# A decoder layer's last stage in 7 tiles of 128 tokens, six batches routed earlier, and two weight loads re-ordered

## The chip, the cores and the metric

The kernel runs on one core of a Trainium2 chip. A core has five engines that run their own instruction queues side by side: TensorE (PE, matmul and transpose), VectorE (DVE), ScalarE (ACT), GpSimd (POOL) and SyncE (SP, which mainly issues DMAs). The metric is the device time of one execution in microseconds (us), as the median of several runs; lower is better.

## The reference, cut to what matters

One decoder layer, post-norm, all in float32, for 8 batches of 112 tokens with 256 channels:

```python
x = _layernorm(x + self_attention(x))        # 16 heads of 64
x = _layernorm(x + cross_attention(x, ctx))  # 16 heads of 16, 375 context tokens per batch, one mask
x = _layernorm(x + ffn(x))

def ffn(x):                                  # x: 896 tokens x 256
    idx = argmax(x @ router.T)               # one of 8 experts for each token
    y = expert[idx](x)                       # silu(x @ gate.T) * (x @ up.T) @ down.T, 512 hidden
    ys = silu(x @ w_gate_s.T) * (x @ w_up_s.T) @ w_down_s.T   # the shared expert, every token
    return y + ys
```

The layernorm has no weights: it subtracts the mean and divides by sqrt(variance + 1e-5).

## The kernel before, in words

**Stages.** The work goes batch by batch. In step s, the self-attention of batch s and the cross-attention of batch s-1 are interleaved; step 0 has no cross-attention, and the last step (table LAST) has the cross-attention of batch 7 and then the feed-forward part. For that the tokens are sorted by expert: the place of each token is counted, its row is sent by an indirect DMA on POOL into a DRAM tensor `xs_d` (`to_places`, L670), each expert's first 128 rows are loaded back (`load_tiles`, L873), go through the expert (`ExpertTile`: `turn` transposes, `gate_up`, `down`), and the output plus its residual goes to `y_d` (L840). A ninth, small tile takes what is beyond 128 rows of an expert; which expert and row that is, SP reads from registers that it loads from memory (L793, L881). At the end the rows of each batch are gathered from `y_d` (`from_places`, L685), the shared expert's product is added, the norm is taken and the rows are written out.

**The order is written by hand.** The scheduler is switched off; each step runs through a table of words, and each engine gets its instructions in that order. A letter is a piece of work: S and E are scores and exponentials of the cross-attention (S, a group of four heads), T its transposes, W and U the weights, V the product with the values, F (or f, of batch 7) the four finishing pieces; s, e, w, t, v, o, n, q are those of the self-attention and of the query projection; k, u, c are projections for later batches. A + or - chooses DVE or ACT for the copy out of PSUM. In LAST, a and b are the shared expert's gate and up products of the first half of the tokens, h those of the second, p (or r) and P (or R) the two halves of the routing (r, R: batches 0 to 5; p, P: batches 6 and 7), L the loads of the sorted rows, A, B, C the turn, gate/up and down of tile 0 to 8, x the count of the rows beyond 128, Y, D, Z the gather, sum and norm of the end. `down(t)` also issues the loads of expert t+4's weights on SP, and for t = 4 the loads of the ninth tile's row number, rows and weights (`load_expert`, L877).

**The start.** SP and ACT's queue issue the first loads (L138 to L148): the first columns of q's weights on ACT, x and k's weights on SP.

**Buffers.** PSUM has two tiles each of three kinds: `sc` (two banks; a cross-attention group S takes both, a self-attention group s takes one), `pt` (transposes) and `mm`. Four sets of expert weights are in flight.

**Every DMA that starts with `load(...)` is issued by SP**, in program order; SP waits for the semaphores of a DMA before it issues it, and what comes later in its queue waits behind.

**The end.** `r`, `mv` are laid out by batch, 112 tokens on the partitions. A batch's norm is one DVE instruction (L242) with the mean and the reciprocal deviation, which POOL makes with a power (L238).

Of the kernel before, what the change touches and what calls it, by code (L numbers as in the profile page):

```python
# [25 lines left out]


STEP = """
S0 E0 k2 s0 u1- e0 T00+ F1 w0 c0 T02- S1 E1 u0- T01+ t00+ W0 s1 T10- T11- e1 c1 T12+ U0+ w1 V0 S2 c4
k3- t01- F2 F3 k0 t10+ t11- E2 v0+ v1- S3 T20+ E3 T22- o W1 T30- c2 n F4 T31+ k1- q1 U1- c3 T21+ q2  # L30
T32- V1
"""
STEP6 = """
S0 E0 c0 s0 c1 e0 T00+ T02- S1 c4 E1 w0 W0 T01- s1 u1- T10- T11- e1 u0+ U0- w1 t00- F1 T12- c3 t01-
S2 t10+ t11- V0 E2 v0+ v1- S3 T20- E3 F2 o n T21- W1 T30- c2 F3 T32- q1 F4 T22- T31- q2 U1+ V1
"""
STEP7 = """
S0 E0 c0 s0 c1 e0 S1 T00- E1 T01+ s1 c4 T02- T10- W0 U0- e1 w0 T12- w1 T11- S2 V0 t00+ t01- E2 F1
t10- v0- t11+ F2 S3 T20- v1+ E3 F3 o T30- n W1 T22- c3 T32- T21+ F4 q1 c2 T31- U1- q2 V1
"""  # L40
FIRST = """
k6 k4 u0- k5- k7+ s0 e0 s1 k3- u3- k1- e1 k2 u1- k0 w0 w1 t00+ t01+ u2- t10+ t11- v0+ v1+ z o c0 n
c1 c3 q1 c4 q2 c2
"""
LAST = """
S0 E0 F1 a2- S1 E1 a1- T00+ b0- T02+ F2 W0 T01- S2 T10+ T12- b1- E2 T11+ U0+ S3 V0 F3 E3 T20+ a3+
T22+ T21+ a0+ W1 T30- T31- F4 T32- U1- r V1 f1 R f2 b2+ f3 f4 b3- p P L0 h2 L1 h0 h1 A0 g1 A1 B0 L2
B1 A2 x C0 B2 A3 A4 C1 C2 B3 B4 A5 A6 C3 B5 C4 B6 A7 C5 B7 g0 A8 C6 B8 C7 C8 Y0 Y1 Y2 Y3 D0 Y4 Y5 D1
h3 Z0 Y6 D2 Z1 Y7 D3 Z2 D4 Z3 D5 Z4 D6 Z5 D7 Z6 Z7
"""  # L50


# [1 line left out]
def decoder_layer(  # L54
# [19 lines left out]
    E, _, H = upT.shape  # L74
    KH = H // P
    NTT = NT // P
    HB = B // 2
    HT = HB * S

    NG = 4  # L80
    NOV = (NT - 1) // P
# [2 lines left out]
    const = ctx.enter_context(tc.tile_pool(name="const", bufs=1))  # L84
# [12 lines left out]
    def m_tile():  # L97
        return ps_m.tile([P, 512], F32, tag="mm", name="mm")
# [10 lines left out]
    ac = sa.enter_context(tc.tile_pool(name="ac", bufs=1))  # L109
# [5 lines left out]
    wo1 = ac.tile([P, NC, D], F32, name="wo1")  # L115
    bo1 = ac.tile([S, D], F32, name="bo1")
    xres = const.tile([S, B, D], F32, name="xres")
    r = const.tile([S, B, D], F32, name="r")
    mv = const.tile([S, B, 2], F32, name="mv")
    x2T = const.tile([P, KD, NT], F32, name="x2T")  # L120
    lgs = const.tile([S, B, E], F32, name="lgs")
    rt = const.tile([P, KD, E], F32, name="rt")
# [1 line left out]
    load = nc.sync.dma_start  # L124
# [3 lines left out]
    def load_w(start, n, c, width):  # L128
        start(out=wqkv[n][:, :, bass.ds(c, width)], in_=w_v[:, :, bass.ds(n * INNER + c, width)])
# [10 lines left out]
        load(out=xT_sb[:, k, 0 : 2 * S], in_=xT_v[:, k, 0 : 2 * S])  # L140
    load_w(A.dma_start, 0, P, P)
    load_w(load, 1, 0, 256)
    load_w(A.dma_start, 0, 256, 256)
    load_w(load, 1, 256, 256)
    for n in range(3):
        load_w(load, n, 512 if n < 2 else 0, 512)
# [64 lines left out]

    xs_d = tc.dram_tile([E * NT, D], F32, name="xs_d")
    y_d = tc.dram_tile([E * NT, D], F32, name="y_d")
    fill_sb = const.tile([P, D], F32, name="fill_sb")
    G.memset(fill_sb, 0.0)

    cap = xc.tile([S, S2], F32, name="cap")
# [9 lines left out]
    def stats(dst, src):  # L227
        st = small.tile([P, 6], F32, tag="st", name="st")
        n = src.shape[0]
        V.bn_stats(st[:n], src)  # L230
        V.bn_aggr(dst, st[:n])

    def rstd_of(var):

        n = var.shape[0]
        rs = small.tile([P, 1], F32, tag="rs", name="rs")
        V.tensor_scalar(rs[:n], var, EPS, None, ALU.add)  # L237
        G.tensor_tensor(rs[:n], rs[:n], mhalf[:n], ALU.pow)  # L238
        return rs[:n]

    def normalize(dst, src, mean, rs):
        V.tensor_scalar(dst, src, mean, rs, ALU.subtract, ALU.mult)  # L242
# [8 lines left out]
    def copy(on, dst, src):  # L251

        (V.tensor_copy if on == "+" else A.copy)(dst, src)  # L253

    def product(out_, pairs):
        for i, (lhsT, rhs) in enumerate(pairs):
            nc.tensor.matmul(out_, lhsT, rhs, start=(i == 0), stop=(i == len(pairs) - 1))  # L257
# [74 lines left out]
    class SelfAttention:  # L332
# [57 lines left out]
        def project(self, on):  # L390
            b = self.b
            G.tensor_tensor(xres[:, b, :], xres[:, b, :], bo1, ALU.add)
            ps = m_tile()
            product(ps[:S, :D], [(self.aoT[:, c, :], wo1[:, c, :]) for c in range(NC)])
            V.tensor_tensor(r[:, b, :], ps[:S, :D], xres[:, b, :], ALU.add)
            stats(mv[:, b, :], r[:, b, :])
            self.rs = rstd_of(mv[:, b, 1:2])

        def norm(self, on):
            b = self.b  # L400
            normalize(xres[:, b, :], r[:, b, :], mv[:, b, 0:1], self.rs)


    class CrossAttention:
# [124 lines left out]
        def finish_3(self):
            transposed(x2T[:, :, bass.ts(self.b, S)], xres[:, self.b, :])  # L530
# [60 lines left out]
    fc = ctx.enter_context(tc.tile_pool(name="fc", bufs=1))  # L591
# [12 lines left out]
    swd = fc.tile([P, KH, D], F32, name="swd")  # L604
# [19 lines left out]
    def shared_half(hc):
        ug = sc_tile()
        for i, w in enumerate((swu, swg)):
            product(
                ug[:, i, :HT], [(w[:, k, bass.ts(hc, P)], x2T[:, k, HT:]) for k in range(KD)]
            )
        sg = fp.tile([P, 512], F32, tag="sg", name="sg", bufs=3)  # L630
        A.activation(sg[:, :HT], ug[:, 1, :HT], AF.Silu)
        V.tensor_tensor(hS1[:, hc, :], ug[:, 0, :HT], sg[:, :HT], ALU.mult)

    rstds = {}

# [2 lines left out]
        A.activation(raw["g"][:, h, :], raw["g"][:, h, :], AF.Silu)  # L638
        V.tensor_tensor(raw["u"][:, h, :], raw["u"][:, h, :], raw["g"][:, h, :], ALU.mult)

    def last_sum(b):

        h = raw["u"] if b < HB else hS1
        ps = m_tile()
        product(
            ps[:S, :D], [(h[:, hc, bass.ts(b % HB, S)], swd[:, hc, :]) for hc in range(KH)]
        )
        V.tensor_tensor(r[:, b, :], ps[:S, :D], r[:, b, :], ALU.add)
# [11 lines left out]
    def small_tile(name, shape=None, dt=F32):  # L660
        return fc.tile(shape or [S, B], dt, name=name)
# [5 lines left out]
    place_i = small_tile("place_i", None, I32)  # L667
# [14 lines left out]
            tc.declare_no_dep(i.ins, other.ins, reason="distinct places")  # L682
        sent.append(i)

    def from_places(b):  # L685
        G.indirect_dma_start(  # L686
            out=r[:, b, :],
            out_offset=None,
            in_=y_d[:, :],
            in_offset=bass.IndirectOffsetOnAxis(ap=place_i[:, b : b + 1], axis=0),  # L690
            bounds_check=E * NT - 1,
            oob_is_err=False,
        )
# [105 lines left out]
    class ExpertTile:  # L799
# [32 lines left out]
        def down(self):  # L832
            ps = m_tile()
            n = self.x.shape[0]
            product(
                ps[:n, :D], [(self.hT[:, hc, 0:n], self.w[2][:, hc, :]) for hc in range(KH)]
            )
            y = fp.tile([P, D], F32, tag="y", name="y", bufs=3)
            V.tensor_tensor(y[:n], ps[:n, :D], self.x, ALU.add)
            load(out=y_d[bass.ds(self.rows, n), :], in_=y[:n])  # L840
# [63 lines left out]
    for b in range(B):
        raw_pieces[f"Y{b}"] = lambda on, b=b: from_places(b)
        raw_pieces[f"D{b}"] = lambda on, b=b: last_sum(b)
        raw_pieces[f"Z{b}"] = lambda on, b=b: last_norm(b)
# [20 lines left out]

    with tc.If(n_more > 0):
        more(0)  # L930
        for b in range(B):
            from_places(b)
            last_sum(b)
            last_norm(b)


# [50 lines left out]
```

## Time and profile before

| what | us |
|---|---|
| median of 3 runs (lowest to highest) | 417.23 (416.98 to 417.66) |
| the profiled execution's own time | 417.91 |
| its span in the profile | 416.1 |
| PE busy / weight loads | 401.2 / 312.9 |
| DVE / ACT / POOL busy | 240.0 / 187.5 / 75.3 |
| PE's first product of q starts / the first waits of the routing (A0) / last expert matmul ends | 4.27 / 339.95 / 388.8 |

The profile is of one execution. A line of the timeline gives start, duration, engine, line of the kernel, operation, output <- inputs, the count of merged instructions, and in brackets how long the engine had been idle and what ended that. A line of waits gives who waited for whom: total us, times, longest. "SPq" and "POOLq" are the sequencers of SP and POOL. A line of a table by stretches gives, for a window of the span, its length, then for PE, weight loads, DVE, ACT and POOL the busy us and the number of instructions, then the granted share of PE's clock, the DMA engines' share and GB/s. Matmul ends are modelled, so the starts are the safer numbers. "To landing" is the time from the issue of a DMA to its completion.

### The profile page before, as it was taken

How to read it: one execution, taken by the hardware profiler on the slowest of the kernel's cores; microseconds unless marked ns; L12 is line 12 of the kernel's file. 1: busy time of each engine (PE TensorE's matmuls, PEld its weight loads, DVE VectorE, ACT ScalarE, POOL GpSimd, SP SyncE). 2: the span in 40 equal slices, each digit the busy share in tenths (PEclk: the TensorE clock that was granted, in tenths of full speed). 3: DMA queues.
4: the chain of work that ended last, by engine and by line, in shares of the span. 5: the costliest groups of instructions: out<-in, count | busy, mean ns of one | idle time of the engine just before them, and what ended most of it. 6: DMA issues, size and time to landing. Idle time of an engine off the chain costs nothing.

```text
span 416.1 us, 8528 instructions
## 1 busy us (share of the span) xinstructions
PE 401.2 (96%) x3361; PEld 312.9 (75%) x3361; DVE 240.0 (58%) x673; ACT 187.5 (45%) x476; POOL 75.3 (18%) x111
## 2 busy tenths in 40 slices
PE   8999999999999999999999999999999999999991
PEld 7877778967886887689678867867857459998670
DVE  1064685578458656855784687498487424223173
ACT  1241475456636554654566386587385221112000
POOL 3021112113012200221130112104100520000271
PEclk9999999999999999999999999999999999999996
DMA  7990497199010001001000100000694140895131
GB/s 258 303 246 0 126 370 253 32 377 334 4 39 0 2 2 38 0 2 38 1 2 2 38 2 2 1 2 2 244 372 144 46 145 2 311 356 171 49 107 56
DMA packets 38622, 46.61 MB, mean 112 GB/s; under 512 B 2213, under 2 KB 31666, under 8 KB 38578
## 3 DMA queue, kind: packets, MB, share of 16 engines
q1 hardware_dynamic: 36994, 43.66, 32.2%
q0 software_dynamic: 768, 1.84, 1.5%
q8 instruction: 28, 0.46, 0.5%
q10 hardware_dynamic: 816, 0.52, 0.4%
q14 instruction: 16, 0.13, 0.1%
HBM read 28.41 MB, written 17.60 MB: 111 GB/s over the span
## 4 chain that ended last, share of the span: by engine, by line
PE 86%; POOL 4%; issue 4%; DMA 3%; DVE 2%; ACT 0%; SPq 0%; POOLq 0%; DVEq 0%
PE mm L257 45%; PE pt L494 10%; PE sc L257 7%; PE sc L446 7%; PE mm L505 5%; PE sc L345 4%; PE mm L381 3%; PE pt L374 3%; POOL r L686 1%; DMA wk<-in_w_qkv 1%; POOL xs_d L673 1%; POOL rs L238 1%; PE pt L248 1%; DMA xs_d<-xres,place_i 1%; PE pt L809 1%
## 5 line engine op out<-in xcount | busy, mean ns | idle before, releaser
L464 ACT ACTIVATE ex<-ex,nm 112x375 f32<-112x375 f32 x128 | 76.5, 599 | 47.6 <-DVE nm L460 46.9
L460 DVE CUSTOM_DVE_ANT_0 ex<-sc,cap 112x375 f32<-112x375 f32 x128 | 63.6, 544 | 10.0 <-PE sc L446 9.6
L494 PEld LDWEIGHTS pt<-ident,ex 112*125 112x125 f32 x384 | 50.9, 188 | 17.1 <-issue 10.0
L494 PE MATMUL pt<-ident,ex 112*125 112x112 f32 x384 | 55.1, 275 | 0.1
L253 ACT COPY exT<-pt 125x448 f32<-125x448 f32 x56 | 28.3, 527 | 29.2 <-PE pt L494 29.1
L367 POOL TENSOR_TENSOR pr<-pr,den 112x896 f32<-112x896 f32 x16 | 26.9, 1683 | 79.5 <-DVE den L366 41.6
L238 POOL TENSOR_TENSOR rs<-rs,mhalf 112x1 f32<-112x1 f32 x24 | 13.4, 559 | 144.6 <-DVE rs L237 144.5
L257 PE MATMUL mm<-wv,xT_sb 128*112 128x512 f32 x64 | 31.1, 608 | 0.0
L446 PE MATMUL sc<-kc,qz 32*112 32x375 f32 x256 | 29.8, 519 | 0.1
L257 PE MATMUL mm<-wo,aoT 128*112 128x256 f32 x128 | 29.0, 380 | 0.0
L253 DVE COPY exT<-pt 125x448 f32<-125x448 f32 x40 | 24.8, 621 | 7.0 <-PE pt L494 6.5
L257 PE MATMUL mm<-xT_sb,wq 128*128 128x224 f32 x128 | 28.3, 367 | 0.0
L257 PE MATMUL mm<-xT_sb,wk 128*128 128x224 f32 x128 | 26.9, 354 | 0.9 <-DMA wk<-in_w_qkv 0.9
L257 PEld LDWEIGHTS mm<-xT_sb,wq 128*128 128x128 f32 x128 | 24.3, 198 | 3.4 <-issue 3.2
L257 PEld LDWEIGHTS mm<-xT_sb,wk 128*128 128x128 f32 x128 | 23.7, 190 | 2.6 <-PE mm L257 1.2
L257 PE MATMUL mm<-wxv,cT 128*125 128x256 f32 x96 | 25.6, 389 | 0.0
L257 PEld LDWEIGHTS mm<-wo,aoT 128*112 128x112 f32 x128 | 22.0, 177 | 4.5 <-DVE aoT L253 0.2
L464 ACT ACTIVATION_READ_ACCUMULATOR ex<-ex,nm 112x1 f32 x128 | 23.9, 187 | 0.0
L257 PE MATMUL mm<-cT,wxk 128*128 128x375 f32 x64 | 23.2, 486 | 0.0
L253 DVE COPY prT<-pt 112x448 f32<-112x448 f32 x16 | 9.8, 620 | 20.7 <-PE pt L374 20.7
L505 PE MATMUL mm<-exT,vc 125*32 125x112 f32 x768 | 21.7, 261 | 0.0
L354 DVE TENSOR_REDUCE mx<-sc 112x8 f32<-112x896 f32 x16 | 17.4, 1087 | 5.8 <-PE sc L345 5.3
(159 smaller groups left out, 647.1 us busy)
## 6 DMA issues: line engine op xcount, KB each, us to landing
xs_d<-fill_sb SPq DMA_DIRECT2D x1, 7168.0 KB, 24.0
y_d<-fill_sb SPq DMA_DIRECT2D x1, 7168.0 KB, 24.7
wg<-in_gateT SPq DMA_DIRECT2D x9, 512.0 KB, 7.2
wu<-in_upT SPq DMA_DIRECT2D x9, 512.0 KB, 7.8
wd<-in_downT SPq DMA_DIRECT2D x9, 512.0 KB, 9.7
cT<-in_ctxT SPq DMA_DIRECT2D x8, 375.0 KB, 3.6
wv<-in_w_qkv SPq DMA_DIRECT2D x2, 512.0 KB, 8.5
wo<-in_w_out SPq DMA_DIRECT2D x1, 1024.0 KB, 12.8
```

The source lines that it names most:

```text
L238: G.tensor_tensor(rs[:n], rs[:n], mhalf[:n], ALU.pow)
L253: (V.tensor_copy if on == "+" else A.copy)(dst, src)
L257: nc.tensor.matmul(out_, lhsT, rhs, start=(i == 0), stop=(i == len(pairs) - 1))
L345: nc.tensor.matmul(sc[:S, j, bass.ts(c, S)], qT[rows, 4 * g + c, self.tok], kT[rows, 4 * g + c, self.tok], start=True, stop=True,)
L354: V.tensor_reduce(self.mx, scv, AX.X, ALU.max)
L367: G.tensor_tensor(pr, pr, den.unsqueeze(3).to_broadcast([S, 2, 4, S]), ALU.mult)
L374: nc.tensor.transpose(pt[:S, bass.ts(c, S)], self.pr[g][:, j, c, :], ident[:S, :S])
L446: nc.tensor.matmul(sc[i // 2][:S, i % 2, :S2], self.qz[rows, par, c, :], kc[rows, c, :], start=True, stop=True,)
L460: V.tensor_tensor_reduce(ex[:, i, :], self.sc[g][i // 2][:S, i % 2, :S2], cap, -1.0, BIG, ALU.add, ALU.min, nm[:, i : i + 1],)
L464: A.activation(ex[:, i, :], ex[:, i, :], AF.Exp, bias=nm[:, i : i + 1], scale=-1.0, accum_out=den[:, i, g % 2 : g % 2 + 1],)
L494: nc.tensor.transpose(pt[:JT, bass.ts(i, S)], self.ex[g][:, i, bass.ts(t, JT)], ident[:S, :S])
L505: nc.tensor.matmul(av[32 * i : 32 * i + 32, 0:S], vcs[self.b % 2][:, t, 4 * c + i, bass.ds(32 * par, 32)], self.exT[2 * c + par][:, t, bas ...
```

## The change

Four things change. (1) The third piece of q's weights (columns 256 to 511) is issued by SP behind the first piece of k's, not by ACT. (2) All tables have a new order. In LAST, routing pieces r and R (the count and the six sends of batches 0 to 5) stand within the cross-attention of batch 7 and no longer behind it; x stands ahead of B1; A8 stands ahead of C5. (3) The last stage runs over 7 tiles of 128 tokens in place of 8 of 112. The places, laid out by batch, are written to a DRAM tensor and read back by tile (pieces i0 and i1, both on SP, behind A5). The split of the shared expert moves from 448 + 448 tokens to 512 + 384. (4) The norm at the end is an ACT instruction, out = r * rstd + shift, with shift = -mean * rstd from a small DVE instruction. Besides, `fill_sb` moves to a pool that is freed earlier. A tail for the case of more rows than the ninth tile holds follows suit; it isn't run with these inputs.

```diff
 STEP = """
-S0 E0 k2 s0 u1- e0 T00+ F1 w0 c0 T02- S1 E1 u0- T01+ t00+ W0 s1 T10- T11- e1 c1 T12+ U0+ w1 V0 S2 c4
-k3- t01- F2 F3 k0 t10+ t11- E2 v0+ v1- S3 T20+ E3 T22- o W1 T30- c2 n F4 T31+ k1- q1 U1- c3 T21+ q2
-T32- V1
+S0 E0 u0+ s0 u1- T00- e0 T01+ S1 E1 k3- s1 c1 T10- e1 T11- w0 k2 T02- k0 W0 w1 t00+ F1 t01- c0 t10+
+U0- c4 T12- t11+ S2 V0 E2 F2 v0+ v1+ S3 T20+ F3 E3 c3 o n W1 F4 T30- T22- k1- T21- q1 c2 T31- T32+
+q2 U1- V1
 """
...
 LAST = """
-S0 E0 F1 a2- S1 E1 a1- T00+ b0- T02+ F2 W0 T01- S2 T10+ T12- b1- E2 T11+ U0+ S3 V0 F3 E3 T20+ a3+
-T22+ T21+ a0+ W1 T30- T31- F4 T32- U1- r V1 f1 R f2 b2+ f3 f4 b3- p P L0 h2 L1 h0 h1 A0 g1 A1 B0 L2
-B1 A2 x C0 B2 A3 A4 C1 C2 B3 B4 A5 A6 C3 B5 C4 B6 A7 C5 B7 g0 A8 C6 B8 C7 C8 Y0 Y1 Y2 Y3 D0 Y4 Y5 D1
-h3 Z0 Y6 D2 Z1 Y7 D3 Z2 D4 Z3 D5 Z4 D6 Z5 D7 Z6 Z7
+S0 E0 a1- b0- T00- r S1 E1 F1 T02- a2- T01+ S2 W0 T10+ R T12- b1- E2 U0+ F2 T11+ a0+ T20- T21+ S3 E3
+V0 T22+ W1 F3 a3+ T30- T31+ F4 T32- U1- V1 f1 f2 b2+ f3 f4 p h1 P h0 h2 L0 b3- L1 A0 A1 B0 L2 x B1
+C0 A2 C1 A3 B2 B3 A4 C2 B4 C3 A5 i0 i1 A6 C4 B5 A7 g1 B6 A8 C5 B7 g0 C6 B8 C7 C8 Y0 Y1 Y2 h3 Y3 Y4
+Y5 D0 D1 Y6 D2 D3 Z0 Z1 D4 D5 Z2 Z3 Z4 D6 Z5 Z6
 """
...
-    HB = B // 2
-    HT = HB * S
+    FT = 4
+    HT, HT2 = FT * P, NT - FT * P
...
-    load_w(A.dma_start, 0, 256, 256)
+    load_w(load, 0, 256, 256)
     load_w(load, 1, 256, 256)
...
-    def last_sum(b):
-
-        h = raw["u"] if b < HB else hS1
+    def last_sum(i):
+
+
+        h, n = (raw["u"], i) if i < FT else (hS1, i - FT)
         ps = m_tile()
-        product(
-            ps[:S, :D], [(h[:, hc, bass.ts(b % HB, S)], swd[:, hc, :]) for hc in range(KH)]
-        )
-        V.tensor_tensor(r[:, b, :], ps[:S, :D], r[:, b, :], ALU.add)
-        stats(mv[:, b, :], r[:, b, :])
-        rstds[b] = rstd_of(mv[:, b, 1:2])
-
-    def last_norm(b):
-        normalize(r[:, b, :], r[:, b, :], mv[:, b, 0:1], rstds[b])
-        load(out=out[bass.ts(b, S), :], in_=r[:, b, :])
+        product(ps[:, :D], [(h[:, hc, bass.ts(n, P)], swd[:, hc, :]) for hc in range(KH)])
+        V.tensor_tensor(r[:, i, :], ps[:, :D], r[:, i, :], ALU.add)
+        stats(mv[:, i, :], r[:, i, :])
+        rstds[i] = rstd_of(mv[:, i, 1:2])
+
+    def last_norm(i):
+        shift = mv[:, i, 0:1]
+        V.tensor_scalar(shift, shift, rstds[i], -1.0, ALU.mult, ALU.mult)
+        A.activation(r[:, i, :], r[:, i, :], AF.Identity, bias=shift, scale=rstds[i])
+        load(out=out[bass.ts(i, P), :], in_=r[:, i, :])
...
+    place_2 = fc.tile([P, NTT], I32, name="place_2")
+
+    def places_out():
+        load(out=place_d[:, :].rearrange("(b s) o -> s (b o)", s=S), in_=place_i)
+
+    def places_in():
+        load(out=place_2, in_=place_d[:, :].rearrange("(i p) o -> p (i o)", p=P))
+
+    def from_places(i):
         G.indirect_dma_start(
-            out=r[:, b, :],
+            out=r[:, i, :],
...
-            in_offset=bass.IndirectOffsetOnAxis(ap=place_i[:, b : b + 1], axis=0),
+            in_offset=bass.IndirectOffsetOnAxis(ap=place_2[:, i : i + 1], axis=0),
```

More of the change, by code (lines that the diff above doesn't have):

```diff
@@ L28 @@
 STEP = """
-S0 E0 k2 s0 u1- e0 T00+ F1 w0 c0 T02- S1 E1 u0- T01+ t00+ W0 s1 T10- T11- e1 c1 T12+ U0+ w1 V0 S2 c4
-k3- t01- F2 F3 k0 t10+ t11- E2 v0+ v1- S3 T20+ E3 T22- o W1 T30- c2 n F4 T31+ k1- q1 U1- c3 T21+ q2
-T32- V1
+S0 E0 u0+ s0 u1- T00- e0 T01+ S1 E1 k3- s1 c1 T10- e1 T11- w0 k2 T02- k0 W0 w1 t00+ F1 t01- c0 t10+
+U0- c4 T12- t11+ S2 V0 E2 F2 v0+ v1+ S3 T20+ F3 E3 c3 o n W1 F4 T30- T22- k1- T21- q1 c2 T31- T32+
+q2 U1- V1
 """
 STEP6 = """
-S0 E0 c0 s0 c1 e0 T00+ T02- S1 c4 E1 w0 W0 T01- s1 u1- T10- T11- e1 u0+ U0- w1 t00- F1 T12- c3 t01-
-S2 t10+ t11- V0 E2 v0+ v1- S3 T20- E3 F2 o n T21- W1 T30- c2 F3 T32- q1 F4 T22- T31- q2 U1+ V1
+S0 E0 c0 s0 c1 e0 T00+ T01- S1 E1 c4 T02- s1 u1- T10- W0 U0- e1 w0 u0- w1 T12- T11- S2 V0 t00- t01-
+F1 t10- t11- E2 v0- v1- S3 F2 E3 T20+ T21+ o W1 n T22- c2 T30- F3 c3 q1 T31- F4 q2 U1+ T32- V1
 """
 STEP7 = """
-S0 E0 c0 s0 c1 e0 S1 T00- E1 T01+ s1 c4 T02- T10- W0 U0- e1 w0 T12- w1 T11- S2 V0 t00+ t01- E2 F1
-t10- v0- t11+ F2 S3 T20- v1+ E3 F3 o T30- n W1 T22- c3 T32- T21+ F4 q1 c2 T31- U1- q2 V1
+S0 c0 E0 s0 c1 e0 S1 T00- E1 T01+ c4 s1 W0 T02- T10- T11- e1 w0 T12- S2 c3 U0- w1 V0 t00- t01- E2 F1
+v0- t10+ F2 t11- S3 v1+ T20+ E3 T21- o T30- T22- n W1 c2 F3 T32- q1 F4 T31- q2 U1- V1
 """
 FIRST = """
-k6 k4 u0- k5- k7+ s0 e0 s1 k3- u3- k1- e1 k2 u1- k0 w0 w1 t00+ t01+ u2- t10+ t11- v0+ v1+ z o c0 n
-c1 c3 q1 c4 q2 c2
+k4 k5- k7- k6 s0 e0 s1 u2- e1 u1+ c1 u3- u0- w0 w1 k1- t00+ c3 z t01- t10- k2 t11+ v0+ v1- o n k3-
+c0 q1 c4 k0 q2 c2
 """
 LAST = """
-S0 E0 F1 a2- S1 E1 a1- T00+ b0- T02+ F2 W0 T01- S2 T10+ T12- b1- E2 T11+ U0+ S3 V0 F3 E3 T20+ a3+
-T22+ T21+ a0+ W1 T30- T31- F4 T32- U1- r V1 f1 R f2 b2+ f3 f4 b3- p P L0 h2 L1 h0 h1 A0 g1 A1 B0 L2
-B1 A2 x C0 B2 A3 A4 C1 C2 B3 B4 A5 A6 C3 B5 C4 B6 A7 C5 B7 g0 A8 C6 B8 C7 C8 Y0 Y1 Y2 Y3 D0 Y4 Y5 D1
-h3 Z0 Y6 D2 Z1 Y7 D3 Z2 D4 Z3 D5 Z4 D6 Z5 D7 Z6 Z7
+S0 E0 a1- b0- T00- r S1 E1 F1 T02- a2- T01+ S2 W0 T10+ R T12- b1- E2 U0+ F2 T11+ a0+ T20- T21+ S3 E3
+V0 T22+ W1 F3 a3+ T30- T31+ F4 T32- U1- V1 f1 f2 b2+ f3 f4 p h1 P h0 h2 L0 b3- L1 A0 A1 B0 L2 x B1
+C0 A2 C1 A3 B2 B3 A4 C2 B4 C3 A5 i0 i1 A6 C4 B5 A7 g1 B6 A8 C5 B7 g0 C6 B8 C7 C8 Y0 Y1 Y2 h3 Y3 Y4
+Y5 D0 D1 Y6 D2 D3 Z0 Z1 D4 D5 Z2 Z3 Z4 D6 Z5 Z6
 """
@@ L117, in decoder_layer @@
     xres = const.tile([S, B, D], F32, name="xres")
-    r = const.tile([S, B, D], F32, name="r")
-    mv = const.tile([S, B, 2], F32, name="mv")
+    r = const.tile([P, B, D], F32, name="r")
+    mv = const.tile([P, B, 2], F32, name="mv")
     x2T = const.tile([P, KD, NT], F32, name="x2T")
@@ L213, in decoder_layer @@
     y_d = tc.dram_tile([E * NT, D], F32, name="y_d")
-    fill_sb = const.tile([P, D], F32, name="fill_sb")
+    place_d = tc.dram_tile([NT, 1], I32, name="place_d")
+    fill_sb = ac.tile([P, D], F32, name="fill_sb")
     G.memset(fill_sb, 0.0)
@@ L394, in project @@
             product(ps[:S, :D], [(self.aoT[:, c, :], wo1[:, c, :]) for c in range(NC)])
-            V.tensor_tensor(r[:, b, :], ps[:S, :D], xres[:, b, :], ALU.add)
-            stats(mv[:, b, :], r[:, b, :])
-            self.rs = rstd_of(mv[:, b, 1:2])
+            V.tensor_tensor(r[:S, b, :], ps[:S, :D], xres[:, b, :], ALU.add)
+            stats(mv[:S, b, :], r[:S, b, :])
+            self.rs = rstd_of(mv[:S, b, 1:2])
         def norm(self, on):
             b = self.b
-            normalize(xres[:, b, :], r[:, b, :], mv[:, b, 0:1], self.rs)
+            normalize(xres[:, b, :], r[:S, b, :], mv[:S, b, 0:1], self.rs)
     class CrossAttention:
@@ L520, in finish_1 @@
             product(ps[:S, :D], [(self.xoT[:, k, :], wx["o"][:, k, :]) for k in range(KD)])
-            V.tensor_tensor(r[:, b, :], ps[:S, :D], xres[:, b, :], ALU.add)
-            stats(mv[:, b, :], r[:, b, :])
-            self.rs = rstd_of(mv[:, b, 1:2])
+            V.tensor_tensor(r[:S, b, :], ps[:S, :D], xres[:, b, :], ALU.add)
+            stats(mv[:S, b, :], r[:S, b, :])
+            self.rs = rstd_of(mv[:S, b, 1:2])
         def finish_2(self):
             b = self.b
-            normalize(xres[:, b, :], r[:, b, :], mv[:, b, 0:1], self.rs)
+            normalize(xres[:, b, :], r[:S, b, :], mv[:S, b, 0:1], self.rs)
         def finish_3(self):
@@ L614, in decoder_layer @@
     raw = {n: fc.tile([P, KH, HT], F32, name=f"raw_{n}") for n in "gu"}
-    hS1 = fc.tile([P, KH, HT], F32, name="hS1")
+    hS1 = fc.tile([P, KH, HT2], F32, name="hS1")
     def shared_raw(on, n, hc):
@@ L627, in shared_half @@
             product(
-                ug[:, i, :HT], [(w[:, k, bass.ts(hc, P)], x2T[:, k, HT:]) for k in range(KD)]
+                ug[:, i, :HT2], [(w[:, k, bass.ts(hc, P)], x2T[:, k, HT:]) for k in range(KD)]
             )
         sg = fp.tile([P, 512], F32, tag="sg", name="sg", bufs=3)
-        A.activation(sg[:, :HT], ug[:, 1, :HT], AF.Silu)
-        V.tensor_tensor(hS1[:, hc, :], ug[:, 0, :HT], sg[:, :HT], ALU.mult)
+        A.activation(sg[:, :HT2], ug[:, 1, :HT2], AF.Silu)
+        V.tensor_tensor(hS1[:, hc, :], ug[:, 0, :HT2], sg[:, :HT2], ALU.mult)
     rstds = {}
@@ L639, in silu_raw @@
         V.tensor_tensor(raw["u"][:, h, :], raw["u"][:, h, :], raw["g"][:, h, :], ALU.mult)
-    def last_sum(b):
-        h = raw["u"] if b < HB else hS1
+    def last_sum(i):
+        h, n = (raw["u"], i) if i < FT else (hS1, i - FT)
         ps = m_tile()
-        product(
-            ps[:S, :D], [(h[:, hc, bass.ts(b % HB, S)], swd[:, hc, :]) for hc in range(KH)]
-        )
-        V.tensor_tensor(r[:, b, :], ps[:S, :D], r[:, b, :], ALU.add)
-        stats(mv[:, b, :], r[:, b, :])
-        rstds[b] = rstd_of(mv[:, b, 1:2])
-    def last_norm(b):
-        normalize(r[:, b, :], r[:, b, :], mv[:, b, 0:1], rstds[b])
-        load(out=out[bass.ts(b, S), :], in_=r[:, b, :])
+        product(ps[:, :D], [(h[:, hc, bass.ts(n, P)], swd[:, hc, :]) for hc in range(KH)])
[7 more added lines that the diff above has]
+        load(out=out[bass.ts(i, P), :], in_=r[:, i, :])
     raw_pieces = {}
@@ L683, in to_places @@
         sent.append(i)
-    def from_places(b):
+    place_2 = fc.tile([P, NTT], I32, name="place_2")
[4 more added lines that the diff above has]
+    def from_places(i):
         G.indirect_dma_start(
-            out=r[:, b, :],
+            out=r[:, i, :],
             out_offset=None,
             in_=y_d[:, :],
-            in_offset=bass.IndirectOffsetOnAxis(ap=place_i[:, b : b + 1], axis=0),
+            in_offset=bass.IndirectOffsetOnAxis(ap=place_2[:, i : i + 1], axis=0),
             bounds_check=E * NT - 1,
@@ L903, in decoder_layer @@
         raw_pieces[f"C{t}"] = lambda on, t=t: down(t)
[L904 to L907, printed above, removed]
+    raw_pieces["i0"] = lambda on: places_out()
+    raw_pieces["i1"] = lambda on: places_in()
+    for i in range(NTT):
+        raw_pieces[f"Y{i}"] = lambda on, i=i: from_places(i)
+        raw_pieces[f"D{i}"] = lambda on, i=i: last_sum(i)
+        raw_pieces[f"Z{i}"] = lambda on, i=i: last_norm(i)
     step(B, LAST, raw_pieces)
@@ L930, in decoder_layer @@
         more(0)
[L931 to L934, printed above, removed]
+        for i in range(NTT):
+            from_places(i)
+            last_sum(i)
+            last_norm(i)
 def kernel(**inputs):
```

## The prediction

> **What bounds the kernel now.** I read the page's busy shares and slices first, then who TensorE (PE) waited for, then the timeline of the start, of the routing and of the end, and last the SyncE (SP) queue. The slices:
>
> ```profile
> PE   8999999999999999999999999999999999999991
> PEclk9999999999999999999999999999999999999996
> ```
>
> PE is busy in every slice up to the last, 401.2 of 416.1 us. So an edit pays in three ways only: fewer microseconds of PE work, one of PE's few waits gone, or a shorter stretch after PE's last matmul. The list of PE's waits says how little the second can give; these are the two large ones:
>
> ```profile
> PE pt L809 <- DMA xs<-xs_d: 0.9, 1, 0.9
> PE mm L257 <- DMA wk<-in_w_qkv: 0.9, 1, 0.9
> ```
>
> The end, from the timeline (start, duration):
>
> ```profile
> 391.86 1.02 POOL L686 DMA_INDIRECT r<-y_d,place_i  x1 [55.68 <-issue]
> ...
> 402.53 1.04 POOL L686 DMA_INDIRECT r<-y_d,place_i  x1 [0.18 <-issue]
> ...
> 407.59 0.42 DVE L648 TENSOR_TENSOR r<-mm,r 112x256 f32<-112x256 f32 x1
> ...
> 409.63 0.41 DVE L242 TENSOR_SCALAR r<-r,mv,rs 112x256 f32<-112x256 f32 x1 [0.44 <-POOL rs L238]
> ```
>
> The last gather lands near 405.4, but its sum starts at 407.59: DVE is behind, with 0.42 sum, 0.43 and 0.18 statistics, 0.15 eps and 0.41 norm per batch. The last expert matmul ends at 388.8 (call it X); SP issues the last output at 410.07, X + 21.27, and 6.0 us of landing and closing follow.
>
> **The parts, against the profiled execution.** The sum stands against its own 417.91 us (span 416.1); the median of the runs is 417.23, so I carry the difference over to 417.23.
>
> *Loads at the start.* PE waits until 7.90 for the first piece of k's weights, which SP issued at 1.75 and which landed 6.0 us later; ScalarE's queue had issued as many bytes of q's (columns 256 to 511) at 1.81, landing 0.2 us after it. With that piece behind k's on one queue, k's lands one transfer earlier: 262 KB at the 314 GB/s of that stretch is 0.83 us, at its slower half-share more. PE ends its first product at 7.00. The moved issue costs SP about 0.5 us, hidden since all later loads wait for bandwidth, not for issue (q's piece is needed at 8.5, about 0.6 us after it landed before). **-0.9** (-0.6 to -0.9; it can't exceed the wait).
>
> *Tables of the steps.* Every piece is the same, so PE's work is. What differs is where matmuls packed on parts of the array (S, s, V, v) stand beside full ones. A q or k piece between two full pieces takes 1.52 us (178.67 to 180.19), between two packed ones 1.71 (160.67 to 162.38): some 0.1 us for each border. The old STEP has 6 full stretches between packed ones, the new 5 (S2 V0 v0 v1 S3 now stand together): 2 x 0.1 x 5 steps = **-0.95**. STEP6, STEP7 and FIRST keep their number (6, 8, 2). Does a wait come in? I followed one STEP by its queues: S1 moves up from 8.6 to 6.5 us after S0, and its second score tile is free at 6.1 (four maxima 1.9 us, max 1.09, subtraction 1.09 on DVE); t00 comes at 15.6 and POOL's 1.68 us product ends at 15.35. Cover of 0.3 us; if it is gone, each 0.1 us costs 0.5 in all. STEP7's old stall at 274.7 (score tiles, same order) stays. 0 (-0.3 to +0.4) for it.
>
> *Six batches sent early.* The six sends (1.25 us apart) leave the queue ahead of the last two; in the new place POOL has only a 0.3 us copy (W1) behind them, due some 1.4 us later. From the last router product (327.03): the old path reaches A0 at 339.95, 12.9 later. New: h1 (8 x 0.32) stands ahead of the count, so it comes 0.6 us later, place after 1.2, two sends, 2.54 landing, 2.11 load: 11.0. PE has 10.3 us of work there. Gain 1.9, but the six raw pieces are 512 wide and not 448 (+0.21 each) and the count stands earlier too: 1.7 us more before. **-0.25** (-0.8 to +0.3).
>
> *The end.* Seven gathers: 1.0 us for 112 rows, up to 1.13 if it grows with the rows; I take 1.05. Six in a row from X + 3.06 at 1.36 spacing, two powers (0.58 each), the seventh at X + 12.3, landing 2.8 later: 15.1. DVE does per tile 0.42 + 0.43 + 0.18 + 0.15 and the new 0.15 shift instead of 0.41, and is level with the gathers: last sum X + 15.45, rstd at 17.5, shift 17.7, ScalarE's norm. For that no row has two pointer operands; the 128x256 copy took 0.37, the exponential with one pointer and 375 elements 0.60; I take 0.55. Issue at X + 18.35: **-2.9** (-2.4 to -3.3). The eighth product group that PE is spared is not on this path. The taller r and mv, the narrower hS1 and fill_sb's other pool are memory alone: 0. Piece x, now ahead of B1, no longer holds C0's output (353.32, though its matmuls ended at 350.2), so expert 4's weights start sooner; PE doesn't wait for them in either order: 0.
>
> *What the round trip of places does.* Pieces i0, i1 turn the places into tiles of 128 through HBM, on SP. i1 reads what i0 wrote, so SP must stand until i0 has landed; that SP does so even for its own queue:
>
> ```profile
> SPq L840 <- DMA y_d<-y: 1.3, 1, 1.3
> ```
>
> Queued behind i1 are C4's output, the ninth tile's register loads, its rows (L883) and its weights. In the old trace:
>
> ```profile
> 358.42 0.48 SPq L840 DMA_DIRECT2D y_d<-y  x1
> ...
> 372.77 0.36 SPq L840 DMA_DIRECT2D y_d<-y  x1
> 375.16 0.36 SPq L883 DMA_DIRECT2D xs<-xs_d  x1
> ```
>
> From output to rows 2.39 us, rows land 1.6 later. And a small transfer lands only behind what is queued before it: the one at 358.42 took 7.3 us, landing 0.35 after the weights ahead. Now the order, from A0's start: first two turns and copy 0.9, gate/up 3.57, down 1.73, turn 0.22. A8 is now ahead of C5 and B7, so it is due at 36.05 (before: 41.35). C3 ends at 26.3, expert 7's weights are issued from 27.3; a set into an idle queue lands 6.5 us on (375.71 to 382.2), so 33.8. i0 lands 0.35 later plus its 896 pieces of 4 bytes, 56 per DMA engine. Nearest row: bq, 8 pieces of 8 bytes per engine, landed 0.25 after the load ahead; seven times that is 1.75. I take 0.6 (0 to 1.75, as most of 0.25 is fixed). i1 at 34.8, C4's output 35.3, rows issued 37.7, landed 39.3: **A8 stalls PE by 3.2** (2.5 to 4.5). Nothing gives it back: PE is the bound up to C8.
>
> *Clock.* A stall that long can also take PE's clock. The windows of the end:
>
> ```profile
> 398.90:402.30 3.40, 2.66 (x13) 1.90 (x12) 1.93 (x8) 0.00 (x0) 3.15 (x4) 1.00 0.45 131
> 405.75:409.16 3.41, 1.25 (x6) 0.71 (x4) 3.20 (x12) 0.00 (x0) 1.31 (x3) 1.00 0.30 85
> 409.16:416.00 6.84, 0.00 (x0) 0.00 (x0) 0.44 (x2) 0.00 (x0) 0.44 (x1) 0.50 0.15 41
> ```
>
> After a stretch in which PE was busy 1.25 of 3.41 us, the granted clock fell to 0.50; after 2.66 of 3.40 it had not. [...] By the row 37% busy is not enough, and 3.2 us idle leaves 6 to 53% of one window: half clock for the next 3.41 us, of which about 0.8 is still stall: 2.6 / 2 = **+1.3**. I take the row.
>
> **Sum.** -0.9 - 0.95 - 0.25 - 2.9 + 3.2 + 1.3 = -0.5: **416.7 us**.
>
> **Rivals.** (a) *The round trip is hidden*: i0 lands early, or A8's rows come in time. Against it speaks the 7.3 us landing, for it that i0 and i1 are only 3.6 KB each. Then -5.0: 412.2. (b) *It costs more, and the kernel is slower*: four-byte writes and reads over 1.5 us each beyond my figure. From 1.4 us later than forecast the whole is over 0.2% slower; at +3 us, 419.7. The unknown piece price speaks for it, the 0.25 us of bq against. (c) *The new STEP waits*: POOL's product for t00 late by 0.5 us beyond its cover, five times 0.5 = 2.5: 419.2 with the rest as forecast. Against: followed by hand it fits. (d) *The clock stays*: 415.4, the near edge of my own case.
>
> **How the numbers follow.** Forecast with or without the clock: 0.56, its own range 414.6 to 418.2; (a) 0.17; (b) 0.17; (c) 0.10. A measurement here tells about 0.2%, 0.83 us (runs spread over 0.7): faster below 416.4, slower above 418.1. Faster: all of (a) and under half of the forecast, 0.42; slower: (b), half of (c) and a little of the forecast, 0.29; same 0.29. The range leaves out the outer half of (a) and of (b): 411.9 to 419.5.
>
> **What would show it.** PE's wait for wk gone; STEP's S0-to-S0 at 38.0 and not 38.2; an SP wait of i1 (the place load) for the place store of some 5 us, and a PE wait of about 3 at L809 for xs late in the experts; a dip of PEclk after it; the last output issued about 18.3 after the last expert matmul. Wrong if A8's wait is under 1 us (then a), or over 5 (b), or if PE shows new waits in the steps (c).

## The result and the profile after

The changed kernel takes 429.61 us (median of 6 runs, 428.91 to 431.46), the kernel before 417.11 (416.40 to 418.04): ratio 1.0303, 95% interval 1.0278 to 1.0328. It is slower by 12.5 us; the forecast was 416.7, its range ended at 419.5. By stretches, from the starts of matmuls in the two profiled executions (spans 416.1 and 428.3; S0 is the first score matmul of a step, A0 the first turn of an expert's rows, X the end of the last expert matmul):

| stretch | before | after | change | forecast |
|---|---|---|---|---|
| start to S0 of step 1 | 46.65 | 45.09 | -1.56 | -0.9 |
| five steps of STEP | 189.61 | 188.85 | -0.76 | -0.95 |
| STEP6 and STEP7 | 63.65 | 63.33 | -0.3 | 0 |
| S0 of LAST to A0 | 40.04 | 45.41 | +5.4 | -0.25 |
| A0 to X | 48.90 | 61.41 | +12.5 | +4.5 (3.2 wait, 1.3 clock) |
| X to the end | 27.27 | 24.20 | -3.1 | -2.9 |

Four rows are near the forecast; two hold the whole miss. The first row differs from one execution to the next: with the same start it is 45.15 to 45.99 in the profiles of experiments 1 to 4 and 7 to 9. The slices of the changed kernel, PE's busy share and its granted clock:

```profile
PE   8999999999999999999999999999978999937991
PEclk9999999999999999999999999999999999975996
```

Before, PE had a 9 in every slice from the second to the last but one. Now there are two holes: one in slices 30 and 31 (310 to 332 us), one in slices 36 and 37 (375 to 396), and behind the second the clock is down as well. The list of PE's waits names both:

```profile
PE pt L820 <- DMA xs<-xs_d: 10.1, 3, 9.5
PE mm L506 <- issue: 2.6, 4, 1.2
```

The wait for `wk` is gone from the list, as forecast. The line of `xs` (L820, which was L809) is the wait at A8, not of 3.2 us but of 9.46. The second line was not in the forecast at all: V0 of the last step (L506) stands still four times, 2.6 us in all, and waits for nothing that the profile can name.

**The second hole: A8.** SP's queue from expert 7's last weights (L602) to the ninth tile's rows (L894):

```profile
372.11 0.41 SPq L602 DMA_DIRECT2D wd<-in_downT  x1
372.56 0.50 SPq L691 DMA_DIRECT2D place_d<-place_i  x1
384.21 0.37 SPq L694 DMA_DIRECT2D place<-place_d  x1
384.68 0.51 SPq L851 DMA_DIRECT2D y_d<-y  x1
386.57 0.36 SPq L894 DMA_DIRECT2D xs<-xs_d  x1
```

Between the second and the third line SP stands for 11.1 us: i1 waits until i0 has landed, 11.6 us after its issue. The chain behind it is the forecast's: i1, C4's output, the ninth tile's rows, A8 at 388.33. A table by stretches (length; busy us and number for PE, weight loads, DVE, ACT, POOL; clock; DMA share; GB/s) shows what the DMA engines did meanwhile:

```profile
370.20:376.50 6.30, 6.30 (x54) 6.14 (x53) 1.12 (x2) 1.48 (x4) 0.00 (x0) 1.00 0.88 270
376.50:378.10 1.60, 1.60 (x17) 1.60 (x16) 1.14 (x1) 0.43 (x1) 0.00 (x0) 1.00 0.67 124
378.10:384.20 6.10, 0.77 (x7) 0.57 (x6) 0.78 (x2) 0.60 (x1) 0.00 (x0) 0.72 0.00 0
380.84:394.50 13.66, 6.17 (x21) 5.42 (x22) 0.42 (x1) 0.21 (x1) 0.00 (x0) 0.50 0.45 137
```

In the first two rows the weights and, among them, the 896 pieces of 4 bytes leave the engines; the last weights' packet starts at 377.70, the last 4-byte one at 378.07. In the third row nothing moves: 0 GB/s for 6.1 us, and only then is i0 reported as landed. The last row is the clock: half speed for 13.66 us, in which PE had 6.17 us of work, so 3.1 us were lost. 9.46 + 3.1 is the 12.5 of the table. The wait varies as well: in experiments 4 to 8, which leave the trip as it is and A8 where it is, it is 7.8 to 8.7 us.

**The first hole: V0.** 48 matmuls that take 1.36 us without a pause. PE's timeline:

```profile
314.58 1.48 PE L506 MATMUL mm<-exT,vc 125*32 125x112 f32 x37
316.54 0.29 PE L506 MATMUL mm<-exT,vc 125*32 125x112 f32 x2 [0.47 <-issue]
317.98 0.27 PE L506 MATMUL mm<-exT,vc 125*32 125x112 f32 x1 [1.15 <-issue]
318.72 0.26 PE L506 MATMUL mm<-exT,vc 125*32 125x112 f32 x1 [0.47 <-issue]
319.43 0.63 PE L506 MATMUL mm<-exT,vc 125*32 125x112 f32 x7 [0.46 <-issue]
```

After 37 matmuls they come singly or in pairs, 0.7 or 1.4 us apart, and the profile shows nothing that they wait for. Below, this is called the dribble. V0 lasts 5.5 us, and the clock is at half from 319.40 to 322.82.

**The end** went as forecast. Gathers, the last sum, the last norm on ScalarE:

```profile
407.02 1.04 POOL L697 DMA_INDIRECT r<-y_d,place  x1 [67.95 <-DMA y_d<-y]
415.90 1.07 POOL L697 DMA_INDIRECT r<-y_d,place  x1 [0.18 <-issue]
419.41 0.42 DVE L648 TENSOR_TENSOR r<-mm,r 128x256 f32<-128x256 f32 x1
421.68 0.60 ACT L655 ACTIVATE r<-r,mv,rs 128x256 f32<-128x256 f32 x1 [0.16 <-DVE mv L654]
```

The last output is issued at X + 18.2 (forecast 18.35, before 21.2).

### The profile page after: what moved, and what is told of

The parts are those of the page before. It is cut to its first block, busy times and chain, and to the rows that moved or that the text cites. A ratio compares the mean times of both kernels' runs of the same rounds, so it can differ in the third digit from the quotient of the medians.

```text
span 428.3 us, 8505 instructions
## 1 busy us (share of the span) xinstructions
PE 403.3 (94%) x3353; PEld 314.6 (73%) x3353; DVE 234.7 (55%) x658; ACT 195.3 (46%) x493; POOL 73.1 (17%) x109
## 4 chain that ended last, share of the span: by engine, by line
PE 85%; DMA 5%; issue 5%; DVE 1%; SPq 1%; POOL 1%; ACT 0%; POOLq 0%; DVEq 0%
PE mm L258 46%; PE pt L495 10%; PE sc L447 6%; PE sc L258 5%; PE mm L506 5%; PE sc L346 4%; PE mm L382 3%; PE pt L375 3%; DMA place_d<-place_i 3%; DMA xs<-xs_d 1%; PE mm L136 1%; DMA r<-y_d,place 1%; PE pt L249 1%; DMA xs_d<-xres,place_i 1%; POOL rs L239 1%
## 5 line engine op out<-in xcount | busy, mean ns | idle before, releaser
L495 PE MATMUL pt<-ident,ex 112*125 112x112 f32 x384 | 54.2, 277 | 0.2 <-ACT exT L254 0.2
L254 ACT COPY exT<-pt 125x448 f32<-125x448 f32 x70 | 36.3, 530 | 23.1 <-PE pt L495 22.9
L239 POOL TENSOR_TENSOR rs<-rs,mhalf 112x1 f32<-112x1 f32 (+1 forms) x23 | 12.6, 552 | 117.0 <-DVE rs L238 116.4
L506 PE MATMUL mm<-exT,vc 125*32 125x112 f32 x768 | 23.2, 262 | 2.6 <-issue 2.6
L506 PEld LDWEIGHTS mm<-exT,vc 125*32 125x32 f32 x768 | 18.2, 110 | 8.8 <-issue 7.7
L254 DVE COPY prT<-pt 112x448 f32<-112x448 f32 x18 | 11.2, 624 | 19.1 <-PE pt L375 19.1
## 6 DMA issues: line engine op xcount, KB each, us to landing
wo<-in_w_out SPq DMA_DIRECT2D x1, 1024.0 KB, 11.6
```

The lines of the kernel that those rows point to most:

```text
L495: nc.tensor.transpose(pt[:JT, bass.ts(i, S)], self.ex[g][:, i, bass.ts(t, JT)], ident[:S, :S])
L506: nc.tensor.matmul(av[32 * i : 32 * i + 32, 0:S], vcs[self.b % 2][:, t, 4 * c + i, bass.ds(32 * par, 32)], self.exT[2 * c + par][:, t, bas ...
```

## The experiments

Two questions. At A8: is i0 slow because of its small pieces (T1), because of what is queued ahead of it, or by a fixed price of a write read back at once (T1')? In V0: is PE short of its next instruction words (T2), or do the six sends on POOL hold it (T2')? The page has a DMA queue for instruction words, `q8 instruction: 28, 0.46, 0.4%`: 28 transfers of 16 KB, one at 314.26. It names no engine. That they are PE's words is the author's estimate; experiment 5, whose edit adds PE instructions alone, has 29 of them.

**1. The trip issued by POOL**

```diff
-load(out=place_d..., in_=place_i)
-load(out=place_2, in_=place_d...)
+G.dma_start(out=place_d..., in_=place_i)
+G.dma_start(out=place_2, in_=place_d...)
```

> The changed kernel with both transfers of the places (i0, i1) issued by POOL and not by SP. Theory T1: PE's 9.5 us wait at A8 is SP standing in its queue until i0's 896 four-byte writes have landed, and the half clock after it (13.65 us, some 3 us lost) comes from that wait; so the wait goes, A0 to the end of C8 returns from 61.3 to about 49 us, and the whole takes about 417. Rival: the small writes slow the DMA engines for everything behind them, whoever issues them; then rows and weights are late all the same and the whole stays above 425.

420.91 us, ratio 1.0084 (1.0053 to 1.0114): between the two expectations. A8's wait is gone, but i0 now goes out as soon as the places are known, at 333.97, just ahead of the loads of the sorted rows. POOL's timeline, then PE's:

```profile
333.97 0.91 POOL L691 DMA_DIRECT2D place_d<-place_i  x1
341.61 1.02 POOL L694 DMA_DIRECT2D place<-place_d  x1 [6.74 <-DMA place_d<-place_i]
```

```profile
341.53 0.69 PE L820 MATMUL pt<-ident,xs 128*128 128x128 f32 x2 [4.42 <-DMA xs<-xs_d]
344.41 0.66 PE L820 MATMUL pt<-ident,xs 128*128 128x128 f32 x2 [2.18 <-DMA xs<-xs_d]
```

i0's 3.5 KB take 7.6 us here, with no weights ahead: the last of its packets ends at 336.13, and 5.5 us pass before the report, near the 6.1 of the trip on SP. The eight loads issued 1.6 us later by SP take 8.0 us in the median, not 2.1. So both theories held a part: SP's standing is gone, and what ran beside the small writes was slow. The wait moved to A0, with 10.24 us of half clock.

**2. A8 late**: `B6 A8 C5 B7 g0` back to `B6 C5 B7 g0 A8`.

> The changed kernel with A8 back behind B7 and g0, where the kernel before has it; the trip of the places is still on SP. By T1 the rows land at the same time, 5.3 us of PE's work now come ahead of A8, and the wait is 9.5 - 5.3 = 4.2 us; half clock for two windows, not four; A0 to the end of C8 about 54 us, the whole about 422. If the rows' wait follows A8 instead (it then stays near 9 us), T1 is wrong.

418.98 us, ratio 1.0040 (1.0020 to 1.0059). A8's wait, again the longest of the line:

```profile
PE pt L820 <- DMA xs<-xs_d: 4.4, 3, 3.7
```

3.7 us against the expected 4.2, the half clock 6.8 us, two windows; A0 to X 55.3. The rows' time doesn't follow A8. The total is 3 us better than expected since V0 ran without a pause (S0 of LAST to A0: 40.05), for which this edit gives no reason.

**3. Whole rows**

```diff
-load(out=place_d[:, :].rearrange("(b s) o -> s (b o)", s=S), in_=place_i)
+load(out=place_d[:, :].rearrange("(s b) o -> s (b o)", s=S), in_=place_i)
```

> The changed kernel with i0 writing 112 whole rows of 32 bytes in place of 896 pieces of 4 bytes; the places then come back in another order, so the end gathers the wrong rows (same number and size). In the trace of the changed kernel the last 4-byte piece had left the DMA engines at about 378.0, and nothing moved until the completion at 384.2. T1, the 6.2 us are spent on the pieces on the memory's side, by their number: with an eighth of the pieces some 0.8 us remain, i0 lands within 1.5 us of the weights ahead of it, A8 waits 3 to 4 us in place of 9.5, and the whole falls by 7 to 9 us. Rival T1', a fixed price of waiting for one's own write: i0 still takes 11 us and A8's wait stays at 9.

424.52 us, 5.1 less than the changed kernel. i0 lands after 5.3 us, at 378.60: 0.5 us after its last piece left the engines at 378.07, not 6.1. SP's queue:

```profile
373.29 0.50 SPq L691 DMA_DIRECT2D place_d<-place_i  x1
378.62 0.37 SPq L694 DMA_DIRECT2D place<-place_d  x1
380.99 0.36 SPq L894 DMA_DIRECT2D xs<-xs_d  x1
```

A8 waits 3.39 us. The gain is short of the expected 7 to 9, but the landing is as T1 has it and T1' falls: same bytes, same queue, same read-back. An eighth of the pieces leaves a twelfth of the silent time. The pieces are also eight times as long and lie side by side in the tensor; whether their number, their length or their place is what costs, this run doesn't tell apart. What remains, 3.4 us, is SP's standing behind the weights: the forecast's own 3.2.

**4. The sends late**: `r` back behind U1, `R` behind f1.

> The changed kernel with r and R back behind V1 and f1. It tells apart two causes of the stretch in V0 of the last step where PE's matmuls come 0.72 us apart with nothing shown that they wait for (2.6 us idle, then half clock). T2, PE is short of its next instruction words, whose refill falls within V0: only 8 PE instructions go from before V0 to behind it, so the stretch stays, first S0 to A0 remains near 45 us and the whole near 429. T2', the six sends on POOL (310.8 to 318.2) and their traffic hold PE: then it vanishes and first S0 to A0 is near 41 us, the whole near 425.

427.88 us. V0 runs through, which spoke for T2'. S0 of LAST to A0 is 41.8, since A0 now waits 2.35 us for rows sent late; that wait brings 3.41 us of half clock too, and the whole is above the 425 of T2'.

**5. More PE instructions at the start**

```diff
+for _ in range(25):
+    nc.tensor.matmul(idle[:32, :32], zeros[:, :32], zeros[:, :32], start=True, stop=True)
```

> The changed kernel with 25 further 32x32 warm-up tiles ahead of everything (about 100 more PE instructions, 1 to 5 us at the start), so that every later refill of PE's instruction words falls at another place of the program; the sends stay early. T2: the dribble in the last step's V0 goes (or turns up at another dense place), and the last step's first S0 to A0 falls from 45.4 to about 41 us. T2': V0 dribbles as before, S0 to A0 stays at 45.4. The A8 wait of 9.5 us stays by both. The whole: 427 to 431 by T2, 431 to 434 by T2'.

423.79 us, below the 427 that even T2 expected; V0 runs through with the sends where the change put them; S0 of LAST to A0 is 40.05. The sends alone therefore don't hold PE. A8 waits 7.8 us.

**6. Fewer PE instructions at the start**: 4 warm-up tiles, not 7.

> The changed kernel with 4 in place of 7 warm-up tiles at the very start (12 fewer PE instructions). The refill of PE's instruction words that went out at V0's first matmul in the changed kernel (314.26, landed 1.19 us later, when V0 had used up 72 instructions in 0.96 us) then goes out when V0 is 12 instructions further on, with less slack. T2: V0 dribbles again, first S0 to A0 of the last step about 45 us. If instead it is clean (40 us), the refill's place isn't what decides. A8's wait stays at 8 to 9.5.

430.07 us; V0 dribbles (five pauses, 2.4 us), S0 of LAST to A0 is 46.7.

**7. The changed kernel once more**, with no edit.

> The changed kernel once more, nothing edited. If the dribble in V0 belongs to the program, first S0 to A0 is 45.4 again and the time 429 to 430.5; if it came with one loading of the program, 40 us and about 425. The wait at A8 is 9 to 9.5 us either way.

429.25 us, V0 with three pauses (3.1 us), 45.6 to A0, A8's wait 8.3. The dribble belongs to the program, not to one loading of it. Experiment 3, too, had it (45.5); experiments 1 and 2 had not, though all these programs are the same on PE up to V0.

**8. Two PE instructions behind everything**

```diff
 def last_sum(i):
...
+    if i == NTT - 1:
+        for _ in range(1):
+            nc.tensor.transpose(t_tile()[:32, :32], ident[:32, :32], ident[:32, :32])
...
```

> The changed kernel with one idle 32x32 transpose on PE behind everything (2 more PE instructions, 75 us after V0 of the last step). So far V0 dribbled in the programs of 6828 and 6816 PE instructions with the sends early and a refill of PE's words at V0's first matmul, and not in those of 6827, 6829 and 6830, equal up to V0. T3, the place of the instruction words in memory (the length of the program behind V0) decides whether the refill is in time: the dribble goes, first S0 to A0 of the last step 40 us, the whole near 425. If it stays (45 us, 429), the length is not it.

424.05 us (two runs). Here V0 is one line without a pause, and S0 of LAST to A0 is 40.1:

```profile
315.08 1.36 PE L506 MATMUL mm<-exT,vc 125*32 125x112 f32 x48
```

No instruction ahead of V0 differs, on any engine, and no wait is shown in it; what differs is the length of PE's program behind it. So the dribble, 5.3 us of the change's 12.5 (S0 of LAST to A0 45.41, here 40.10), is not the price of a wait or a transfer that the change put ahead of V0. The supply of instruction words (T2), whose place in memory the added instructions could shift, is what is left of the two causes asked about. That is argued: no trace shows a shift or a late word. Nor does the length alone decide, since experiment 4 has as many PE instructions as the changed kernel (6828, with 8 of them moved behind V0) and no pause.

**9. The places turned by PE, written in 8 rows, trip on POOL**

```diff
-load(out=place_d[:, :].rearrange("(b s) o -> s (b o)", s=S), in_=place_i)
+place_t = fp.tile([B, S], I32, tag="sg", name="place_t", bufs=3)
+V.tensor_copy(top, place_i)
+pt = t_tile()
+nc.tensor.transpose(pt[:B, :S], top, ident[:S, :S])
+V.tensor_copy(place_t, pt[:B, :S])
+G.dma_start(out=place_d[:, :].rearrange("(b s) o -> b (s o)", s=S), in_=place_t)
...
-load(out=place_2, in_=place_d[:, :].rearrange("(i p) o -> p (i o)", p=P))
+G.dma_start(out=place_2, in_=place_d[:, :].rearrange("(i p) o -> p (i o)", p=P))
```

The copies use `top` and a buffer of `sg`: with two tiles of its own, this form was 0.31 KB a partition too large for SBUF (pool `wp`: 48 KB a partition, 47.69 left).

> The changed kernel with the places turned by PE first (one 112x8 transpose in i0, two small DVE copies), so that i0 writes 8 rows of 448 bytes, and both transfers issued by POOL, which has nothing else to do between the sends and the gathers. By T1 (the 896 four-byte writes are what is slow) nobody waits for it: A8's wait under 0.5 us, A0 to the end of the last expert matmul about 49 us in place of 61.4, no half clock there, i0 lands within 3 us of its issue. With the dribble in V0 as in the changed kernel the whole is about 417, without it 412 to 413.5, below the kernel before by 3.5 to 5. If a write read back at once has a fixed price (T1'), i0 still takes 6 us or more to land, though hidden.

413.31 us, ratio to the kernel before 0.9908 (0.9893 to 0.9923): faster than both. Slices, waits and POOL:

```profile
PE   8999999999999999999999999999999899999991
PEclk9999999999999999999999999999999999999998
```

```profile
PE pt L825 <- DMA xs<-xs_d: 0.8, 2, 0.6
PE pt L694 <- DVE top L692: 0.5, 1, 0.5
```

```profile
365.61 0.58 POOL L696 DMA_DIRECT2D place_d<-place_t  x1 [31.95 <-DVE place_t L695]
371.11 1.01 POOL L699 DMA_DIRECT2D place<-place_d  x1 [4.91 <-DMA place_d<-place_t]
```

A0 to X is 49.75, no half clock before the end, and A8's wait is gone. i0 takes 5.5 us to land (expected 3), but its eight packets leave the engines only between 369.16 and 370.02, beside weights at 308 GB/s. So 3.5 us are the way to the engines, and the silence before the report is 1.1 us. Nobody waits for it: the gathers start at 390. V0 runs through (40.07). With the same two idle instructions behind it:

> The kernel with the transposed trip on POOL (6830 PE instructions, no dribble, 413.3 us) with one idle 32x32 transpose on PE behind everything (6832). T3: if it goes by the length modulo 4, V0 dribbles here: first S0 to A0 45 us, the whole about 417.5. If not, the whole stays at 413.3 to 413.5 and the dribble is none of the length's.

413.88 us, V0 again without a pause (39.9). The programs with pauses had 6828 and 6816 PE instructions, both multiples of 4; this one has 6832, so that is not the rule either. What sets the dribble off stays open.

**10. Two parts alone, on the kernel before**

> The kernel before with only the one edit that q's third piece is issued by SP behind k's first. By the prediction PE's wait of 0.90 us for k's first weights goes and nothing else moves: -0.9 us, 416.2. Rival: what PE gains there it loses at a later piece of the start that now lands later (q's third piece); then under 0.3 us.

> The kernel before with only the new table STEP. By the prediction 0.1 us for each packed stretch fewer beside full ones, two sides, five steps: -0.95 us (the trace of the changed kernel showed 0.15 per step, 0.76 in all); about 416.2. Rival: new waits in the steps; then the time is the same or up to 2.5 us longer.

The loads: 416.45, ratio 0.9983 (0.9977 to 0.9990), -0.7 us. The table: 416.33, ratio 0.9979 (0.9972 to 0.9987), -0.8 us; each of its steps is 0.15 us shorter, with no new wait.

## Why the prediction was wrong

**The term that failed** is i0's landing: "0.35 later plus its 896 pieces ... I take 0.6 (0 to 1.75, as most of 0.25 is fixed)". By the trace the weights' last packet came at A0 + 35.0 (forecast 33.8), the pieces left the engines 0.4 later, and then 6.1 us passed before the write was reported. That most of 0.25 is fixed was an estimate, and no run shows it. So the wait of 3.2 became 9.46: 1.2 from later weights (the set took 7.5 us from its first issue, at 370.23, and not 6.5), 5.5 from the pieces, and 0.5 back because SP came from i1 to the rows in 2.4 and not 2.9 us. Everything else of that chain was right: A8 was due at A0 + 36.2 (forecast 36.05), rows landed 1.6 us after issue.

The row that I took as nearest, bq's, has pieces nearly as small (8 bytes) but goes the other way: it reads from HBM and writes to SBUF. i1 reads the same 896 pieces of 4 bytes from HBM and on SP's queue lands 2.3 to 3.1 us after its issue, which is about what the sorted rows take (2.1); on POOL's it took 5.2 and 6.6 (experiments 1 and 9). Of i0 and i1 on SP's queue only i0, the write to HBM, was dear: 6.1 us / 896 is about 7 ns for each piece after the engines had sent them (an estimate, as if they went one after another); a bound of 1.75 from a read could not hold them. In experiment 3, 112 pieces of 32 bytes left 0.5 us; what is done with a piece in that time no run shows.

**The clock term** (+1.3) had the beginning right and the length wrong. The clock halved behind a window in which PE was busy 1.44 of 3.41 us, as the row that I took says. But it didn't come back when PE did:

```profile
377.43:380.84 3.41, 1.44 (x13) 1.24 (x12) 1.45 (x2) 0.60 (x1) 0.00 (x0) 1.00 0.06 5
387.67:391.08 3.41, 2.75 (x8) 2.27 (x9) 0.00 (x0) 0.21 (x1) 0.00 (x0) 0.50 0.87 278
391.08:394.50 3.42, 3.42 (x15) 3.15 (x14) 0.42 (x1) 0.00 (x0) 0.00 (x0) 0.50 0.66 228
```

Two windows passed with PE idle (0.00 us busy from 380.84 to 387.67), then one with PE busy for 2.75 us, and only behind one with PE busy throughout was the clock full again. All 14 half-clock stretches inside these traces go so: PE is busy at most 1.6 us in the window before, at most 3.0 in every window of the stretch but the last, and throughout (3.38 us or more) in the last. So the term was too small even for the wait of the forecast: in experiment 3, with a wait of 3.39 us, two windows passed at half clock with 5.56 us of work in them, a loss of 2.8 us and not 1.3.

**V0 was no term at all**, and no rival held it. It cost 5.3 to 5.5 us (S0 of LAST to A0 is 45.41, 45.54 and 45.58 in the changed kernel and experiments 3 and 7, and 40.05 to 40.10 in 2, 5, 8 and 9). Without it the changed kernel would still be 1.6% slower (experiment 8); without the trip's cost but with the dribble it would be near 419 (413.3 + 5.4, an estimate). The trace has the 16 KB transfers of instruction words, and one starts 0.3 us ahead of V0, which starts 73 instructions in its first 0.9 us; that transfer took 1.19 us. But in experiments 1, 2, 4, 8 and 9, without a pause, one starts 0.2 to 0.3 us ahead of V0 as well and takes 0.96 to 1.15 us. So its time doesn't tell the cases apart, and the cause of the dribble stays open.

**What held.** STEP's borders: -0.95 forecast, -0.76 in the trace, no new waits, so rival (c) falls. Loads: -0.9 forecast, -0.7 in time (experiment 10); in experiments 6 and 8 a wait of 0.8 us for `wk` was there all the same, so it is a gain of most executions, not of all. STEP6 and STEP7 were 0 and gave 0.3. The early sends: S0 of LAST to A0 is 40.05 to 40.1 without the dribble, 40.04 before, so 0 and not -0.25. The end: -3.1 for -2.9; ScalarE's norm took 0.60 (forecast 0.55), the shift 0.2 (0.15).

**The rivals.** (b) is what happened, beyond its own size: it was priced at +3 us and came at 6.3 of wait and 1.8 of clock above the forecast. (a) was worth 412.2; experiment 9, which makes it true, takes 413.3, and 0.85 of the difference is A0 to X (49.75, before 48.90) with the transpose and PE's wait for it. (d) is out: the clock went.

## What to carry to other kernels

Count the pieces of a small transfer, and take their price from a row that goes the same way: here 896 writes of 4 bytes to HBM took 6.1 us after the engines had sent them, and reading them back on SP's queue took 2.3 to 3.1 us in all, about what the loads of the sorted rows took. Turn such data on an engine first, so that the write is a few rows (8 rows of 448 bytes took 1.1 us after the engines had sent them), and give a round trip to a queue behind which nobody stands (on POOL, experiment 9: A0 to X 49.75 us, not 61.41). Before a loss in one stretch is put down to an edit, compare with a kernel that is the same up to there: 5.3 us here went with two idle instructions at the other end of the program. Price a lost clock up to the end of the first window in which PE is busy throughout, not up to the end of the wait: here 13.65 us of half clock in whole windows of 3.41 us, for a wait of 9.46.

## What was not expected of the hardware

- 896 writes of 4 bytes to HBM: 6.1 us between the last packet and the report (5.5 when POOL issued them); 112 of 32 bytes: 0.5 us; 8 of 448 bytes, beside the weights: 1.1 us. While the 4-byte writes were in flight (experiment 1), loads of 128 KB took 8.0 us in the median, not 2.1.
- A dense stretch of PE, V0's 96 matmuls and weight loads in 1.36 us, stood still for 2.4 to 3.1 us with no wait shown, in steps of about 0.7 us, in both profiles of one program (2.6 and 3.1 us), and not for one that is two instructions longer behind it.
- Half clock at A8 lasted 13.65, 10.24 and 6.83 us with waits of 9.46, 8.3 and 3.7 us (the changed kernel, experiments 7 and 2): whole multiples of 3.41 us. With a wait of 7.8 us (experiment 5) it was 6.83 again: in these runs the number of windows followed from when PE was first busy for a whole one (3.38 us or more), not from the wait alone.
